# Layer 0 attention: each query and key part written to DRAM once, and repeated by the reads that fetch the rows back

## The chip, the core and the metric

The kernel runs on one core of a Trainium2 chip. A core has five engines with instruction queues of their own: PE (matrix products), DVE (vector), ACT (activation functions), POOL (general vector work, and the DMAs it issues) and SP (which here only issues DMAs). Sixteen DMA engines move data between DRAM and the on-chip memory; all queues share them. The metric is the device time of one execution in microseconds (us), lower is better.

## The reference, cut to what matters

Two transformer layers on 8 sequences (batches) of 256 rows of width 128. Each layer is a cross-attention with a residual, and a top-2 mixture of 8 experts with a residual. The change touches only the attention of layer 0: 16 heads of 8 columns each, whose scores get a hash mask.

```python
def _L0_xattn_ref(query, key, value, hash_q, hash_k, Wq, bq, Wk, bk, Wv, bv):
    q = _split_heads(query @ Wq.T + bq, B, Lq)      # 16 heads of 8
    k = _split_heads(key @ Wk.T + bk, B, Lk)
    v = _split_heads(value @ Wv.T + bv, B, Lk)
    scores = jnp.einsum('bhqd,bhkd->bhqk', q, k) / jnp.sqrt(jnp.float32(D_K))
    mask = (hash_q[:, :, :, None] != hash_k[:, :, None, :]).astype(scores.dtype) * NEG
    attn = jax.nn.softmax(scores + mask, axis=-1)
    out = jnp.einsum('bhqk,bhkd->bhqd', attn, v)
    return out.transpose(0, 2, 1, 3).reshape(B, Lq, D_MODEL)
...
x = x + _L0_xattn_ref(_layernorm(x), ctx_1024, ctx_1024, mask, mask, ...)
x = x + _L0_ffn_ref(_layernorm(x), ...)
x = x + _L1_xattn_ref(_layernorm(x), ctx_1024, ctx_1024, ...)
x = x + _L1_ffn_ref(_layernorm(x), ...)
```

## The kernel before, in words

**The operands of a score.** A float32 query or key value is split into three bf16 parts (`part`, lines 433 to 439) whose sum is the value. A float32 product is then the sum of 3 x 3 products of parts. The kernel puts all nine into one contraction: of the 128 partitions of the tiles `q9` and `k9` (one row of 16 heads x 256 positions, 8 KB in bf16, per partition), rows 0 to 71 hold (i, j, d), i and j the part numbers and d one of the 8 columns of a head. Row (i, j, d) of `q9` is part i of the query's column d, and row (i, j, d) of `k9` is part j of the key's. Rows 72 and 73 hold the hash mask (`mrow`), and rows 74 to 76 of `q9` the row maxima in three parts, `mT`, against rows of minus one in `k9`. So every part of the query stands in `q9` three times, and the same holds for the key. `q9` and `k9` have three buffers each: batch b uses number b % 3.

**prep0(b)** (line 422) makes these tiles for a batch: layer norm, the two projections, the split into parts, the value projection, four small DMAs for the mask rows (line 455), and then the rows of parts. The part tile has (column, head) on its partitions, while `q9` needs columns on partitions and heads along the row, so the rows go through a DRAM tile `rows`. For batch 0 eighteen DMAs go straight from `part` to `q9` and `k9` instead (line 467). For the others there are six writes of 192 KB (line 475), each of which writes all three parts of the query or of the key to one of the three places where they are repeated, and then two reads of 72 rows x 8 KB, 576 KB each, one into `q9` (line 478) and one into `k9` (line 479). All of these DMAs stand in SP's queue.

**The loop.** Layer 0's attention is one loop over n (lines 1083 to 1110), in which an iteration does two heads of scores for one half of the queries (`scores`, line 490 on PE, and the maximum over the keys on DVE, line 494), and, 15 iterations later, one head of probabilities (`probs`: the transposed scores with the maxima subtracted, line 521 on PE, exponential on ACT, line 528). A batch takes 16 iterations. Every iteration ends with `tick()`, which moves each generator in the list `side` on to its next `yield`; `prep0(b + 2)` is put there in iteration 2 of batch b. With its yields its mask rows are issued around the end of batch b, its writes from iteration 1 of batch b + 1 on, and its reads four ticks after the first writes.

**maxima(b, half)** (line 496) splits the maxima of eight heads into three parts, transposes them on PE, copies them on ACT (line 513) and puts them into rows 74 to 76 of `q9` by a DMA from SP, `q<-mT` (line 514). The first half of batch b (heads 0 to 7) is due in iteration 10 of b, the second half (heads 8 to 15) in iteration 2 of batch b + 1. The first `probs` of the second half, head 8, stands at iteration 7 of batch b + 1: it waits for that DMA.

**What sets the order.** PE, ACT, DVE and SP run their instructions in the order in which the program text issues them. SP's queue takes one DMA at a time: an instruction that waits holds all behind it. A read of `rows` waits until the writes of its data have landed. There are eight completion semaphores for SP's DMAs, which are used in turn, so that a DMA also waits for the eighth before it. POOL issues weight loads for later stages during the loop (`load_later`, line 250), each behind a DVE maximum.

**Another place of use.** `tails` (line 708) fills rows of a DRAM table: eight times per layer SP issues a DMA of 80 rows of 1040 float32 numbers, whose source is 16 rows repeated five times by a broadcast (line 722, `xs<-blank`, 325 KB).

Of the kernel before, what the change touches and what calls it, by code (L numbers as in the profile page):

```python
# [12 lines left out]
BF16 = mybir.dt.bfloat16  # L13
# [6 lines left out]
S = 256  # L20
QT = S // P
D = 128
H = 16
DK0 = 8
# [27 lines left out]
NPART = 3  # L52
R_MASK = NPART * NPART * DK0
# [9 lines left out]
def kernel(  # L63
# [28 lines left out]
    nc = tc.nc  # L92
# [4 lines left out]
    dp = ctx.enter_context(tc.tile_pool(name="dp", bufs=3, space=bass.MemoryType.DRAM))  # L97
# [7 lines left out]
    def bank(tag, name, dt=F32):  # L105

        if tag == "any":
            third.append(third.pop(0))
            tag = third[-1]
        return ps.tile([P, 512 * 4 // mybir.dt.size(dt)], dt, tag=tag, name=name, bufs=1 if tag in ("pv", "y") else 2)  # L110
# [77 lines left out]
    with nc.allow_non_contiguous_dma(reason="two rows of biases, once"):  # L188
        for i, src in enumerate((bq0, bk0)):
            nc.scalar.dma_start(  # L190
                out=brow[:, i, :].rearrange("o (d g j) -> o d g j", d=DK0, g=4),
                in_=src.rearrange("(o j z) g -> o z g j", o=1, z=32)[:, :DK0],
# [188 lines left out]
    def norm_T(tiles, name, rows=None, lead=2):  # L381
        n = len(tiles)
        mv = sm.tile([P, GT, 2], F32, tag="mv", name=f"mv{name}", bufs=3)
        for i, t in enumerate(tiles):
            st = sm.tile([P, 6], F32, tag="bn", name=f"st{name}_{i}", bufs=3)
            nc.vector.bn_stats(out=st, in_=t)
            nc.vector.bn_aggr(out=mv[:, i, :], in_=st)
            if i == 1 and n > 2:
                yield
        ve = sm.tile([P, GT], F32, tag="ve", name=f"ve{name}", bufs=3)  # L390
        nc.vector.tensor_scalar(ve[:, :n], mv[:, :n, 1], EPS, None, ALU.add)
        rs = sm.tile([P, GT], F32, tag="rs", name=f"rs{name}", bufs=3)
        nc.gpsimd.tensor_tensor(rs[:, :n], ve[:, :n], mhalf[:, :n], ALU.pow)
        for _ in range(lead):
            yield
        xns = []
        for i, t in enumerate(tiles):
            if rows is None:
                xn = sm.tile([P, D], F32, tag="xn", name=f"xn{name}_{i}", bufs=4)
                to = xn  # L400
            else:
                xn = rows[:, i, 0, :D]
                to, t = rows[:, i, :, :D], t.unsqueeze(1).to_broadcast([P, 2, D])
            nc.vector.tensor_scalar(to, t, mv[:, i, 0:1], rs[:, i : i + 1], ALU.subtract, ALU.mult)
            xns.append(xn)
            if i == 1 and n > 2:
                yield
        for _ in range(1 if rows is None else 2):
            yield
        pt = bank("pt", f"np{name}")  # L410
        for i, xn in enumerate(xns):
            nc.tensor.transpose(pt[:, ts(i, P)], xn, ident)
        tag, bufs = (f"xnT{n}", 2) if rows is None else (f"xnTr{n}" if n == QT else f"xnT{n}", 1)
        xnT = wk.tile([P, n * P], F32, tag=tag, name=f"xnT{name}", bufs=bufs)
        nc.scalar.copy(xnT, pt[:, : n * P])
        yield
        return xnT
# [4 lines left out]
    def prep0(b):  # L422
        q9, k9, v = q9s[b % 3], k9s[b % 3], v0s[b % 4]
        xnT = yield from norm_T(xt[b * QT : (b + 1) * QT], f"a{b}", lead=6 if b >= 2 else 2)
        pq = bank("pt", f"pq0_{b}")
        nc.tensor.matmul(pq[:, :S], lhsT=wq0_sb, rhs=xnT, start=True, stop=True)
        nc.tensor.matmul(pq[:, S:], lhsT=wk0_sb, rhs=ct[b], start=True, stop=True)
        f = wk.tile([P, 2, S], F32, tag="g2", name=f"qk{b}", bufs=5)
        nc.scalar.activation(f[:, 0, :], pq[:, :S], AF.Identity, bias=bqk[:, 0:1], scale=1.0 / math.sqrt(DK0))
        nc.scalar.activation(f[:, 1, :], pq[:, S:], AF.Identity, bias=bqk[:, 1:2])  # L430
        yield

        part = wk.tile([P, NPART, 2, S], BF16, tag="pT", name=f"part{b}")
        rest = wk.tile([P, 2, S], F32, tag="g2", name=f"rest{b}", bufs=5)
        eng = nc.vector if b < 2 else nc.gpsimd
        eng.tensor_copy(part[:, 0], f)
        eng.tensor_tensor(rest, f, part[:, 0], ALU.subtract)
        eng.tensor_copy(part[:, 1], rest)
        eng.tensor_tensor(part[:, 2], rest, part[:, 1], ALU.subtract)
        yield  # L440
        pv = bank("pt", f"pvp0_{b}")
        for t in range(QT):
            nc.tensor.matmul(pv[:, ts(t, D)], lhsT=ct[b][:, ts(t, P)], rhs=wv0_sb, start=True, stop=True)
        nc.vector.tensor_tensor(
            v[:, :, :, :DK0],
            pv[:, : QT * D].rearrange("p (t h d) -> p t h d", t=QT, d=DK0),
            bv0_sb.rearrange("p (h d) -> p h d", d=DK0).unsqueeze(1).to_broadcast([P, QT, H, DK0]),
            ALU.add,
        )
        yield  # L450
        for _ in range(2 if b >= 2 else 0):
            yield
        for t, k in ((q9, 0), (k9, 2)):
            for i in range(2):
                nc.sync.dma_start(
                    out=t[R_MASK + i : R_MASK + i + 1, :, :], in_=mrow[b * H : (b + 1) * H, k + i, :]
                )
            yield
        if b == 0:

            queues = [nc.sync, nc.scalar, nc.sync, nc.scalar, nc.gpsimd]
            for i in range(NPART):
                for j in range(NPART):
                    r = (i * NPART + j) * DK0
                    for n, t in ((0, q9), (1, k9)):
                        queues.append(queues.pop(0))
                        queues[-1].dma_start(out=t[r : r + DK0, :, :], in_=part[:, (i, j)[n], n, :])
            yield
            return

        rows = dp.tile([2, R_MASK, H, S], BF16, tag="rows", name=f"rows{b}")
        for n, by in ((0, "(i j d) h s -> j (d h) i s"), (1, "(i j d) h s -> i (d h) j s")):
            to = rows[n].rearrange(by, i=NPART, j=NPART)
            for i in range(NPART):
                nc.sync.dma_start(out=to[i], in_=part[:, :, n, :])
                if b > 1 and i:
                    yield
        nc.sync.dma_start(out=q9[:R_MASK, :, :], in_=rows[0])
        nc.sync.dma_start(out=k9[:R_MASK, :, :], in_=rows[1])
        yield  # L480

    def scores(b, i):
# [579 lines left out]

    mrow = wk.tile([P, 4, S], BF16, tag="ns", name="mrow", bufs=4)
    first = prep0(0)
    next(first)
    next(first)
# [7 lines left out]
    tick()  # L1074
    tick()
    side.append(prep0(1))
    drain()
    for i in range(3):
# [4 lines left out]
    for n in range(NS * B + LAG + 3):  # L1083
        b, i = divmod(n, NS)
        if n < NS * B:
            scores(b, i)
        if 0 <= n - LAG < H * B:
            probs(*divmod(n - LAG, H))
        g, r = divmod(n - LAG - 5, 4)
        if r == 0 and 0 <= g < 4 * B:  # L1090
            values0(*divmod(g, 4))
            if g % 2:
                side.append(finish0(g // 4, g % 4 // 2))
        if i in (HH, 0) and HH <= n <= NS * B:
            side.append(maxima((n - 1) // NS, 1 if i == 0 else 0))
        if i == 2 and b + 2 < B:
            side.append(prep0(b + 2))
        if i == 6 and b in (3, 5, 7):
            one_by_one(route(0, 2 * (b - 3), GT, nc.gpsimd))
            if b == 7:  # L1100
                one_by_one(place(0, True))
                one_by_one(route(0, NT - 2 * QT, QT))
        if n == NS * B + 8:
            side.append(keys_values(0))
        tick()
        if n == NS * B + LAG - 2:
            begin0(range(4))
            tiles0 = run0()
        if n >= NS * B + LAG:
            next(tiles0)  # L1110
# [94 lines left out]
```

## Time and profile before

| | us |
|---|---|
| median of 3 runs | 771.52 |
| lowest and highest | 765.64, 774.53 |
| the profiled execution, its own time | 772.35 |
| its span (first to last instruction) | 770.6 |

The profile is of one execution; its own time is 1.75 us over its span, and 0.8 us over the median. The busy shares of the span: PE 82%, DVE 62%, ACT 43%, POOL 42%; the granted TensorE clock was 0.904 of full speed on average.

The stages by time: set-up to 39.8 us, the loop of layer 0's attention from there to about 243 us, layer 0's experts to about 350 us, layer 1's attention to about 630 us, layer 1's experts and the combination to the end. In a line of a timeline, the first two numbers are the start and the duration in us; SPq is SP's queue and its duration is that of issuing, not of the transfer; what stands in brackets is the idle time before and what ended it. In a table of windows each engine has its busy time and its instruction count, and the last three columns are the granted clock of PE, the share of the 16 DMA engines that was busy, and GB/s.

### The profile page before, as it was taken

The numbers are of one execution on the slowest core, as the hardware profiler recorded it, in microseconds if no ns is written. First come the engines' busy times: TensorE is split into PE (matmuls) and PEld (weight loads), VectorE is DVE, ScalarE is ACT, GpSimd is POOL, SyncE is SP. The second block draws the span as 40 slices with busy tenths as digits, with TensorE's granted clock in tenths as the row PEclk, the third lists the DMA queues.
The fourth block names the chain that finished last, engine by engine and source line by source line (L and its number), as shares of the span: only waits on it lengthen the run. The fifth ranks groups of instructions, "written<-read, shape, count | busy, mean of one in ns | idle before, by whom it ended". The sixth has DMA issues, their size and how long they took to land. (4 is left out here: it accounts for less than half of the span.)

```text
span 770.6 us, 15199 instructions
## 1 busy us (share of the span) xinstructions
PE 631.4 (82%) x4781; PEld 487.1 (63%) x4781; DVE 478.3 (62%) x1804; ACT 333.0 (43%) x1028; POOL 325.9 (42%) x393
## 2 busy tenths in 40 slices
PE   2179889686876689998899999999999773979990
PEld 1135454353533679997578777777768663879990
DVE  4177787774834465554857778778786783444442
ACT  1015564443632122223675656656575550423330
POOL 4044547534060354443533444536353740454442
PEclk9956997987967799999999999999999997899995
DMA  3657876754015455662203020000000015758845
GB/s 90 57 157 220 227 188 198 166 147 121 3 63 163 118 142 154 195 168 68 68 1 90 27 77 16 16 15 16 1 15 1 15 38 173 219 157 227 232 135 170
DMA packets 72758, 83.85 MB, mean 109 GB/s; under 512 B 9648, under 2 KB 55624, under 8 KB 71672
## 3 DMA queue, kind: packets, MB, share of 16 engines
q1 hardware_dynamic: 63840, 63.79, 30.7%
q0 software_dynamic: 7600, 18.64, 8.0%
q10 hardware_dynamic: 1240, 0.46, 0.7%
q8 instruction: 39, 0.64, 0.3%
q14 instruction: 39, 0.32, 0.1%
HBM read 60.86 MB, written 30.60 MB: 119 GB/s over the span
## 5 line engine op out<-in xcount | busy, mean ns | idle before, releaser
L945 ACT ACTIVATE p<-ns,nm 128x256 f32<-128x256 f32 (+1 forms) x256 | 114.4, 450 | 33.7 <-DVE nm L934 29.0
L958 POOL TENSOR_TENSOR p<-p,rd 128x1024 f32<-128x1024 f32 (+1 forms) x63 | 92.1, 1482 | 63.6 <-DVE rd L953 62.4
L817 POOL DMA_INDIRECT ys<-yj,xj x78 | 75.1, 963 | 89.9 <-DVE yj L815 80.3
L494 DVE TENSOR_REDUCE mx<-sc 128x2 f32<-128x512 f32 x128 | 84.1, 685 | 33.2 <-PE sc L490 24.6
L656 POOL DMA_INDIRECT xs<-rows,ati x64 | 63.2, 987 | 90.8 <-DVE rows L648 45.6
L528 ACT ACTIVATE pT<-st 128x512 f32<-128x512 f32 x128 | 73.9, 596 | 60.9 <-PE st L521 56.5
L934 DVE CUSTOM_DVE_ANT_0 ns<-s,tri 128x256 f32<-128x256 f32 (+1 forms) x256 | 77.1, 350 | 0.5 <-PE s L919 0.5
L490 PE MATMUL sc<-k,q 74*128 74x256 bf16 x256 | 57.7, 315 | 19.8 <-DVE mx L494 9.4
L970 ACT COPY pT<-pt 128x512 f32<-128x512 f32 x64 | 36.9, 576 | 70.2 <-PE pt L968 70.2
L521 PE MATMUL st<-q,k 77*128 77x256 bf16 x256 | 56.8, 311 | 8.4 <-DMA q<-mT 4.4
L968 PE MATMUL pt<-ident,p 128*128 128x128 f32 x384 | 58.1, 280 | 4.7 <-POOL p L958 3.2
L968 PEld LDWEIGHTS pt<-ident,p 128*128 128x128 f32 x384 | 46.3, 143 | 23.9 <-DVE k L885 11.4
L983 PE MATMUL o<-pT,v 128*64 128x256 f32 (+1 forms) x512 | 54.2, 335 | 5.0 <-ACT pT L970 3.3
L796 DVE TENSOR_TENSOR h<-s,pu 128x256 f32<-128x256 f32 x78 | 23.9, 348 | 52.0 <-PE pu L790 21.7
L780 ACT ACTIVATE h<-ph,wj 128x128 f32<-128x128 f32 x78 | 24.5, 365 | 71.7 <-issue 51.4
L777 PE MATMUL ph<-xT,wj 128*128 128x128 f32 x312 | 47.5, 299 | 9.2 <-DVE xT L764 5.7
L919 PE MATMUL s<-k,q 64*128 64x256 f32 (+1 forms) x512 | 53.2, 338 | 0.5 <-DVE nm L934 0.5
L490 PEld LDWEIGHTS <-q 74*128 74x128 bf16 x256 | 24.8, 109 | 43.7 <-issue 38.2
L983 PEld LDWEIGHTS o<-pT,v 128*64 128x64 f32 x512 | 34.9, 137 | 23.7 <-issue 6.2
L919 PEld LDWEIGHTS s<-k,q 64*128 64x128 f32 x512 | 42.8, 186 | 10.3 <-issue 4.5
L945 ACT ACTIVATION_READ_ACCUMULATOR p<-ns,nm 128x1 f32 x256 | 49.2, 192 | 0.0
L777 PEld LDWEIGHTS ph<-xT,wj 128*128 128x128 f32 x312 | 40.7, 203 | 11.6 <-DVE xT L764 6.2
(218 smaller groups left out, 1289.8 us busy)
## 6 DMA issues: line engine op xcount, KB each, us to landing
wj<-wa SPq DMA_DIRECT2D x39, 352.0 KB
wj<-wa SPq DMA_DIRECT2D x39, 258.0 KB
rows<-part SPq DMA_DIRECT2D x42, 192.0 KB
xs<-blank SPq DMA_DIRECT2D x16, 325.0 KB
xj<-xs SPq DMA_DIRECT2D x78, 65.0 KB
yy<-ys SPq DMA_DIRECT2D x16, 256.0 KB
q<-rows SPq DMA_DIRECT2D x7, 576.0 KB
k<-rows SPq DMA_DIRECT2D x7, 576.0 KB
```

The source lines that it names most:

```text
L490: nc.tensor.matmul(sc[:, k, :], lhsT=q9s[b % 3][:R_MAX, h, ts(qt, P)], rhs=k9s[b % 3][:R_MAX, h, :], start=True, stop=True,)
L494: pace[0] = nc.vector.tensor_reduce(c0[b]["mx"][:, qt, 2 * u : 2 * u + 2], sc, AX.X, ALU.max)
L528: nc.scalar.activation(pT.rearrange("p t s -> p (t s)"), st, AF.Exp)
L656: nc.gpsimd.indirect_dma_start(out=xs[l][:, :], out_offset=to, in_=rows[:, i, k, :], in_offset=None),
L777: nc.tensor.matmul(phs[z][:, ts(i, P)], lhsT=wj[:, o : o + P], rhs=xT, start=True, stop=True)
L817: free(f"ys{l}", nc.gpsimd.indirect_dma_start(out=ys[l][:, :], out_offset=to, in_=yj, in_offset=None))
L919: nc.tensor.matmul(u["s"][a, r][:, (1 - qt) * S : (1 - qt) * S + n], lhsT=c1[b]["q"][rows, c, ts(qt, P)], rhs=c1[b]["k"][rows, c, :n], sta ...
L934: nc.vector.tensor_tensor_reduce(out=ns[:, o : o + n], in0=s[:, o : o + n], in1=tri[:, S - n :], scale=-1.0, scalar=3.0e38, op0=ALU.add, o ...
L945: nc.scalar.activation(p[:, o : o + n], ns[:, o : o + n], AF.Exp, bias=nm[:, a : a + 1], scale=-1.0, accum_out=u["sum"][:, 2 * i + a : 2 * ...
L958: eng.tensor_tensor(p, p, rd[:, :, a : a + 1].to_broadcast([P, 4, n]), ALU.mult)
L968: nc.tensor.transpose(pt[:, ts(n, P)], u["p"][:, i, (S, 0, P)[m] :][:, :P], ident)
L983: nc.tensor.matmul(o[DK1 * r : DK1 * (r + 1), a, t * P :], lhsT=v[:, t, cols], rhs=pT, start=(t == 0), stop=True, skip_group_check=True,)
```

## The change

In `prep0`, for all batches but 0: the DRAM tile `rows` becomes a third as large and holds each part of the query and of the key once. Two writes of 192 KB take the place of six, and there is one `yield` after them. The repetition moves into the reads: the query's rows come in three DMAs, one for each i, of 24 rows each, whose source is the 8 rows of part i repeated three times by a broadcast of step 0; the key's come in one DMA of 72 rows whose source is its 24 rows repeated three times. The bytes that the reads bring in are as before, 576 KB for each of the two tiles. The yields between the writes are gone.

```diff
-        rows = dp.tile([2, R_MASK, H, S], BF16, tag="rows", name=f"rows{b}")
-        for n, by in ((0, "(i j d) h s -> j (d h) i s"), (1, "(i j d) h s -> i (d h) j s")):
-            to = rows[n].rearrange(by, i=NPART, j=NPART)
-            for i in range(NPART):
-                nc.sync.dma_start(out=to[i], in_=part[:, :, n, :])
-                if b > 1 and i:
-                    yield
-        nc.sync.dma_start(out=q9[:R_MASK, :, :], in_=rows[0])
-        nc.sync.dma_start(out=k9[:R_MASK, :, :], in_=rows[1])
+        rows = dp.tile([2, NPART, DK0, H * S], BF16, tag="rows", name=f"rows{b}")
+        for n in range(2):
+            nc.sync.dma_start(
+                out=rows[n].rearrange("i d (h s) -> (d h) i s", h=H), in_=part[:, :, n, :]
+            )
+        yield
+        for i in range(NPART):
+            nc.sync.dma_start(
+                out=q9[i * NPART * DK0 : (i + 1) * NPART * DK0, :, :],
+                in_=rows[0][i].unsqueeze(0).to_broadcast([NPART, DK0, H * S]),
+            )
+        nc.sync.dma_start(
+            out=k9[:R_MASK, :, :],
+            in_=rows[1].rearrange("j d w -> (j d) w").unsqueeze(0).to_broadcast([NPART, NPART * DK0, H * S]),
+        )
         yield
```

## The prediction, made before the changed kernel was run

> **What bounds the kernel now.** I read the page's slices first, then windows of the loop of layer 0's attention (39.8 to about 243 us), then SP's and PE's timelines there.
>
> ```profile
> PE   2179889686876689998899999999999773979990
> DMA  3657876754015455662203020000000015758845
> xs<-blank SPq DMA_DIRECT2D x16, 325.0 KB
> rows<-part SPq DMA_DIRECT2D x42, 192.0 KB
> ```
>
> Slices of 19.3 us: in the loop (slices 3 to 12) PE is mostly at 8 to 9 tenths and the DMA engines at 5 to 8. The stage runs at PE's pace, and since PE takes its instructions in order, a wait on PE is paid in full unless PE would have idled later.
>
> ```profile
> core 0: us, PE busy (x) PEld busy (x) DVE busy (x) ACT busy (x) POOL busy (x), PEclk, DMA share, GB/s
> 43.00:44.00 1.00, 0.16 (x1) 0.00 (x0) 0.93 (x6) 0.00 (x0) 0.37 (x1) 0.50 0.76 197
> 56.50:76.40 19.90, 19.67 (x133) 11.55 (x131) 14.05 (x37) 11.40 (x22) 9.40 (x15) 0.66 0.79 219
> 76.40:92.20 15.80, 15.30 (x148) 9.41 (x147) 13.46 (x38) 10.65 (x22) 8.37 (x12) 1.00 0.84 243
> 634.00:644.00 10.00, 8.22 (x69) 6.59 (x65) 4.87 (x17) 1.55 (x3) 0.72 (x1) 1.00 0.32 127
> ```
>
> Last three columns: granted clock, busy share of the 16 DMA engines, GB/s. At 43 us little but a read of 72 plain rows runs: share 0.76, so about 12 engines of 16, at 197/12 = 16.4 GB/s each. From 634 to 644 us it is almost only `xs<-blank`, whose source is a broadcast of five: share 0.32, so 5 engines, at 127/5 = 25 GB/s each. The other eleven idle while SP's queue has more for them.
>
> ```profile
> 57.78 1.58 SPq L475 DMA_DIRECT2D rows<-part  x3
> 60.44 0.80 SPq L514 DMA_DIRECT2D q<-mT  x1
> 61.28 1.60 SPq L475 DMA_DIRECT2D rows<-part  x3
> 64.02 0.33 SPq L478 DMA_DIRECT2D q<-rows  x1
> 66.28 0.32 SPq L479 DMA_DIRECT2D k<-rows  x1
> 86.19 0.31 SPq L479 DMA_DIRECT2D k<-rows  x1
> 89.89 0.78 SPq L514 DMA_DIRECT2D q<-mT  x1
> ```
>
> ```profile
> 65.58 0.64 PE L521 MATMUL st<-q,k 77*128 77x256 bf16 x2
> 95.86 0.38 PE L521 MATMUL st<-q,k 77*128 77x256 bf16 x2 [2.78 <-DMA k<-mrow]
> 154.19 0.39 PE L521 MATMUL st<-q,k 77*128 77x256 bf16 x2 [2.94 <-DMA q<-mT]
> 167.31 0.39 PE L521 MATMUL st<-q,k 77*128 77x256 bf16 x2 [1.48 <-DMA q<-mT]
> ```
>
> The SP rows are one preparation (batch 2) and the end of the next. `q<-mT` at 60.44 is the second half of batch 0's maxima; head 8 of batch 0 needs it, at 65.58. It stands between the writes, ahead of the reads. `q<-mT` at 89.89 is a first half; it stands behind the k read of 86.19, and head 0 of batch 2 starts only at 95.86, after 2.78 us of idling (the page puts that on `k<-mrow`, long done). So an `mT` behind the big reads lands when they have, about 5.9 us after its issue here, while one with nothing big ahead (152.06, needed at 154.19) takes 2.1.
>
> **The change part by part.**
>
> *Four writes fewer for each of 7 batches.* A write keeps all DMA engines busy for about 0.7 us: at 40 to 42 us the share is 1.05 with 290 GB/s, and 192 KB at that rate is 0.68 us. So 28 x 0.7 = 19 us of DMA time go, and 28 issues of 0.5 us on SP. Neither is what PE waits for: no score of batches 1 to 7 waits for `q<-rows` or `k<-rows`. Worth 0 by itself; the cover is the slack of 9 to 10 us between a k read's issue (66.28) and its first score (76.38).
>
> *The reads move up.* They followed the sixth write, two to four iterations later; now they follow the second. In the built program SP's order for a batch is: four mask rows, two writes, four reads, then the second half's `mT`. Before, the `mT` stood ahead of the reads (even ahead of the last three writes). So what waits behind the reads changes from the first half's `mT` to the second half's. Gain: the waits of 2.78 and 1.48 us, about 4 us.
>
> *The reads themselves.* Here row and rule part from the plain estimate. Row: 2 x 576 KB = 1.18 MB at 197 GB/s is 6.0 us. But a broadcast source ran on 5 engines for a broadcast of five. The Trainium skill, "DMA: Bandwidth & Descriptors", section "Rules for kernel authors", says why: a DMA runs on the largest number of engines, up to 16, that divides the slowest dimension of both access patterns, so a leading broadcast of c copies confines it to c engines. The row of 0.32 agrees for c = 5. All four new reads lead with a broadcast of 3: three engines, 144/3 = 48 rows of 8 KB each. At 25 GB/s a row is 0.33 us: 16 us. Bounds: at 16.4 GB/s per engine (the 43 us row) 24 us; nothing in the trace moves more than about 25 GB/s on an engine, so hardly under 15. I take 16, as few engines are the nearer row, plus 2 us for POOL's loads, which share these engines (estimate: the loop's 219 GB/s less the rows' traffic leaves about 2 MB in 20 us, 5 us of each engine; PE's wait stops the loads, which go behind DVE's maxima, so I take less than half). The skill's page also says that these are the lowest-numbered engines; an `mT`, 3 rows, then uses the same three, and queues behind the reads as it did at 89.89.
>
> *When the second half lands.* With W the issue of a batch's first write: the first read can go once that write has landed, 3.2 us (a k read follows the last write by 2.4 to 3.4 us); 1.7 us to the first data (the q read of 41.39 is seen at 43); 18 us of reads. The `mT` lands at W + 23. Head 8 of the batch in question starts, before, after W by:
>
> W = 57.78, 79.07, 95.00, 119.19, 147.82, 168.21; head 8 = 65.58, 84.11, 104.60, 129.36, 154.19, 177.63; distances 7.8, 5.0, 9.6, 10.2, 6.4, 9.4, together 48.4.
>
> Six stalls of PE, 6 x 23 - 48.4 = 90 us. Behind the waiting `st` on PE stand the next scores, so DVE, ACT and POOL's pacing stop with it. Batches 6 and 7 have no preparation and no stall.
>
> *Start.* Batch 1's reads begin at about 42.5 and hold the three engines to about 58.5. Behind them in SP's queue are the nine `k<-minus`, the eighth of which waits for the k read's semaphore (eight in turn), and then batch 0's first `mT`, issued at about 60 instead of 53.74, landed at 62; head 0 of batch 0 started at 56.13: +6 us. The first scores, at 39.8, are untouched.
>
> *Clock.* After each stall PE restarts at half speed. Rule: "TensorE: Matmul & The Clock Gate", Part 1, the clock halves when PE idles for more than about 3.4 us, and a stretch of PE work would take up to twice as long. Row: the 16 score iterations at 0.66 mostly (56.56 to 75.43) took 18.9 us, those at 1.00 (76.38 to 92.2) 15.8; half speed costs 0.2 to 0.3 us an iteration, not double. By the rule 6 x 5 us or more, by the row about 6 x 1.5 = 9 us; I take the row.
>
> *Given back.* DVE and POOL catch up during stalls: PE's waits of 6.5 us before 186.8 (ACT's `oT`) and 2.7 at 141.6 (DVE) may go. -8 us.
>
> The tails, layer 1 and the experts are as before and start later by the sum: 90 + 6 + 9 - 4 - 8 = **+93 us**. The profiled execution is 772.35, so 865; it lies 0.8 over the median, which changes nothing.
>
> **The rivals.**
>
> *Twelve engines after all* (the compiler or queue spreads the repeated rows over their 24 or 72). Then only the order changes: reads 6 + 2 us, `mT` at W + 13.2, stalls 79 - 48 = 31, less 4 and less 8, no start term: about +19, 791 us. For: the destination has 24 and 72 rows. Against: `xs<-blank` has 80 rows and still ran on 5 engines.
>
> *Faster:* the reads are early and harmless, and only the waits at the first halves go: -4 to -7, 767 us. One mechanism: the second `mT` has to land before head 8, within 5 to 10 us of W, of which 5.2 are latency; that leaves at most 5 us for 1.18 MB, 236 GB/s from these reads alone, decided at that rate. Against: no read of rows came near it (197).
>
> *Three engines at the slow rate:* 24 us of reads instead of 16, 6 x 8 = 48 more and 8 at the start: 921 us. For: 8 KB rows took the slow rate on twelve engines. Against: five engines with repeated rows had 25 GB/s each, and at 43 us the twelve may have slowed each other, which three would do less.
>
> **How the numbers follow.** Three engines near 25 GB/s 0.82: 865. Slow rate 0.09: 921. Twelve engines 0.05: 791. Faster or unchanged 0.04: 767. The likeliest gives the time. Its own range is 822 (15 us, no interference by POOL, a larger share given back) to 910; to leave out no more than 2 in 10, the upper end goes to 915, and the low end stays at 820, as twelve engines and the harmless cases together are 0.09. About 1% (8 us) is what a measurement of this kernel tells from no change; faster 0.03, within 1% 0.02, slower 0.95.
>
> **What would show it.** In the loop of the new profile: DMA share near 0.2 to 0.3 for some 16 us after each pair of writes, at about 75 GB/s; PE idle at `st<-q,k` six times for 12 to 18 us until `q<-mT`, at heads 8 of batches 0 to 5, and about 6 us at the first head; no such wait in batches 6 and 7; half clock after each. Wrong if the reads show a share of 0.7, or if the waits are at the scores instead, or if the stages after the loop change length.

## The result: slower by an eighth

The changed kernel takes 867.09 us (median of four runs, 865.18 to 868.97). The kernel before, run beside it, takes 773.02 us (765.64 to 778.54). The ratio is 1.125, with an interval of 1.116 to 1.134. It is not the quotient of the two medians because it leaves out a slow run of the kernel before, 778.54 (the mean of its other three runs is 770.56). The prediction was 865 us in a range of 820 to 915. The profiled execution took 867.82 us, over a span of 866.1 us, which is 95.5 us more than the span before.

The page of the changed kernel: busy tenths in 40 slices of 21.7 us, then two of the costliest groups (busy time and mean of one; after the second bar, the idle time before them and what ended most of it).

```profile
PE   2243825544373876779998999999999977579990
...
PEclk9555858667776967899999999999999999698996
DMA  3523314151412014456623022000000002656865
...
L500 DVE TENSOR_REDUCE mx<-sc 128x2 f32<-128x512 f32 x128 | 83.7, 683 | 128.0 <-PE sc L496 126.3
L527 PE MATMUL st<-q,k 77*128 77x256 bf16 x256 | 57.4, 313 | 109.8 <-DMA q<-mT 108.7
```

The loop of layer 0's attention (slices 2 to 15) shows PE at 8 tenths in two slices and at 2 to 7 in the others. PE and the DMA engines are both low in most of them: nobody is the bottleneck by its amount of work. The line numbers are six higher than before: L527 is the `st` matmul of `probs`. It idled for 108.7 us until `q<-mT` had landed. DVE idles with it (128.0 us), because the scores that it reduces stand behind the waiting `st` on PE.

PE's timeline, lines with that wait (start, duration, and in brackets the idle time before and what ended it):

```profile
64.33 0.59 PE L527 MATMUL st<-q,k 77*128 77x256 bf16 x2 [9.14 <-DMA q<-mT]
88.07 0.60 PE L527 MATMUL st<-q,k 77*128 77x256 bf16 x2 [15.13 <-DMA q<-mT]
123.49 0.61 PE L527 MATMUL st<-q,k 77*128 77x256 bf16 x2 [17.04 <-DMA q<-mT]
160.53 0.61 PE L527 MATMUL st<-q,k 77*128 77x256 bf16 x2 [17.75 <-DMA q<-mT]
203.50 0.61 PE L527 MATMUL st<-q,k 77*128 77x256 bf16 x2 [17.91 <-DMA q<-mT]
241.74 0.61 PE L527 MATMUL st<-q,k 77*128 77x256 bf16 x2 [17.17 <-DMA q<-mT]
278.50 0.61 PE L527 MATMUL st<-q,k 77*128 77x256 bf16 x2 [14.56 <-DMA q<-mT]
```

The first is head 0 of batch 0. The six others are heads 8 of batches 0 to 5, together 99.6 us. Batches 6 and 7, which have no preparation of another batch beside them, have no such line.

SP's timeline around the first of the six, with the queue's order as the prediction gave it: two writes, three reads of the query's rows, one of the key's, then the `mT` that head 8 at 88.07 waits for, 16.8 us after its issue.

```profile
42.58 19.57 SPq L333 DMA_DIRECT2D k<-minus  x9
...
62.25 0.78 SPq L520 DMA_DIRECT2D q<-mT  x1
...
65.58 1.06 SPq L473 DMA_DIRECT2D rows<-part  x2
67.83 2.25 SPq L478 DMA_DIRECT2D q<-rows  x3
70.50 0.68 SPq L482 DMA_DIRECT2D k<-rows  x1
71.28 0.74 SPq L520 DMA_DIRECT2D q<-mT  x1
```

Windows of the changed kernel, two within the waits and three behind the first of them (last three columns: granted clock, busy share of the 16 DMA engines, GB/s):

```profile
76.00:87.00 11.00, 0.00 (x0) 0.00 (x0) 0.00 (x0) 0.00 (x0) 0.00 (x0) 0.50 0.19 78
110.00:121.00 11.00, 0.00 (x0) 0.00 (x0) 0.00 (x0) 0.00 (x0) 0.00 (x0) 0.50 0.19 80
...
88.00:91.00 3.00, 2.93 (x22) 1.32 (x22) 1.75 (x7) 1.19 (x2) 0.56 (x1) 0.50 0.00 0
91.00:94.00 3.00, 3.00 (x22) 2.14 (x18) 1.87 (x6) 2.04 (x4) 0.00 (x0) 0.87 0.28 87
94.00:97.00 3.00, 3.00 (x33) 1.85 (x32) 1.51 (x4) 2.04 (x5) 2.23 (x3) 1.00 0.27 90
```

For 11 us no compute engine does anything, while 0.19 of 16 engines, that is three, move 78 to 80 GB/s, about 26 GB/s each. Thirteen DMA engines stand by.

Where the 95.5 us of span went can be added up from the timelines: until the first `st` (56.34 before, 64.33 after) 8.0; from there to the last `st` (242.4 before, 335.9 after) 186.1 become 271.6, which is 85.5; from there to the end 528.2 become 530.2, which is 2.0.

### The profile page after: what moved, and what is told of

It reads as the page before. It is cut to its first block, busy times and chain, and to the rows that moved or that the text cites. A ratio compares the mean times of both kernels' runs of the same rounds, so it can differ in the third digit from the quotient of the medians.

```text
span 866.1 us, 15178 instructions
## 1 busy us (share of the span) xinstructions
PE 632.6 (73%) x4781; PEld 487.5 (56%) x4781; DVE 478.1 (55%) x1804; ACT 332.0 (38%) x1028; POOL 325.9 (38%) x393
## 5 line engine op out<-in xcount | busy, mean ns | idle before, releaser
L500 DVE TENSOR_REDUCE mx<-sc 128x2 f32<-128x512 f32 x128 | 83.7, 683 | 128.0 <-PE sc L496 126.3
L527 PE MATMUL st<-q,k 77*128 77x256 bf16 x256 | 57.4, 313 | 109.8 <-DMA q<-mT 108.7
L527 PEld LDWEIGHTS <-k 77*128 77x128 bf16 x256 | 27.3, 110 | 121.7 <-DMA q<-mT 101.2
L496 PE MATMUL sc<-k,q 74*128 74x256 bf16 x256 | 57.5, 315 | 18.9 <-DVE mx L500 11.6
```

The lines of the kernel that those rows point to most:

```text
L496: nc.tensor.matmul(sc[:, k, :], lhsT=q9s[b % 3][:R_MAX, h, ts(qt, P)], rhs=k9s[b % 3][:R_MAX, h, :], start=True, stop=True,)
L500: pace[0] = nc.vector.tensor_reduce(c0[b]["mx"][:, qt, 2 * u : 2 * u + 2], sc, AX.X, ALU.max)
L527: nc.tensor.matmul(st[:, ts(t, S)], lhsT=k9s[b % 3][:R_ALL, h, ts(t, P)], rhs=q9s[b % 3][:R_ALL, h, :], start=True, stop=True,)
```

## The experiments

Each kernel computes the whole. Its ratio is to runs of the kernel before on the same chip in the same session; that kernel took 768.67 us beside the first four, 749.12 beside the next three and 771.92 beside the last, so the ratios are what to compare, not the times.

### The mT from another queue

```diff
-        nc.sync.dma_start(out=q9s[b % 3][R_MAX:R_ALL, ts(hf, HH), :], in_=mT)
+        nc.scalar.dma_start(out=q9s[b % 3][R_MAX:R_ALL, ts(hf, HH), :], in_=mT)
```

> The changed kernel, with the maxima rows q<-mT issued from ACT's queue instead of SP's; reads, engines and places as in the changed kernel. Theory (the second half's q<-mT is held because it stands behind three-engine reads in the same queue): from another queue it lands in 2 to 4 us although the reads run on the same engines, so the six waits of 101 us at head 8 shrink below 10 in all. Left are about 7 us at the first head (k<-minus still stands behind batch 1's reads) and new, small waits of the scores for reads that land 22 us after the first write (they are needed 17 to 26 us after it: some 10 us in all): 780 to 795 us. Rival (three crowded DMA engines hold every DMA that uses them, whatever its queue): still 855 to 870.

Measured: 825.96 us, ratio 1.071 (1.061 to 1.082), between the two ranges and in neither. PE's waits from 30 to 345 us (total, times, longest):

```profile
PE sc L496 <- DMA q<-mrow: 25.2, 2, 18.9
PE st L527 <- DMA q<-mT: 23.9, 8, 6.4
PE sc L496 <- DMA k<-rows: 12.1, 1, 12.1
```

The stalls at `st` shrank from 108.7 to 31.2 us: the 23.9, and 7.3 at the first head, which stand under `k<-minus` in this profile. So most of the wait was the place in the queue. Not all of it: an `mT` that PE waited for took 3.3 to 9.7 us here from its issue by ACT to the waiting `st` (105.03 to 111.22 and 130.44 to 140.14, for instance), against 15.3 to 21.6 us in SP's queue, and against the 2 to 4 us that were expected. The rival, that the crowded engines hold every DMA, fits that part; no run here singles it out.

The scores now wait for rows in the loop, 18.9 and 12.1 us (6.3 of the first line are at the start, where the kernel before waits too, 8.0 us). SP's timeline of this kernel shows why, for the first of the two, which ends at 98.63:

```profile
70.85 1.06 SPq L473 DMA_DIRECT2D rows<-part  x2
78.62 2.25 SPq L478 DMA_DIRECT2D q<-rows  x3
80.97 0.69 SPq L482 DMA_DIRECT2D k<-rows  x1
```

The q reads go out 7.8 us after the writes; in the changed kernel it was 2.3 us (65.58 and 67.83), and the writes themselves were 5 us earlier. Something holds SP's queue now. The last experiment looks at that.

### The reads four ticks later

```diff
-        yield
+        for _ in range(4 if b > 1 else 1):
+            yield
         for i in range(NPART):
```

> The changed kernel with its four reads issued four ticks after the two writes, as the kernel before had them, so behind the second half's q<-mT; still three engines. Theory: the waits at head 8 go, and come back smaller at head 0, where the first half's q<-mT now stands behind reads that take about 19 us from their issue and is needed about 12 us after it: six waits of 2 to 10 us, some 40 us, and 7 at the start: 815 to 830 us. Rival (the cost is the length of the reads alone, wherever they stand): 860 to 870. Rival (the cost is the place alone): 770 to 780.

Measured: 827.53 us, ratio 1.073 (1.064 to 1.083), as expected. The second half's `mT` is now ahead of the reads, and the first half's behind them. PE's timeline has the stalls at heads 0 instead of heads 8: five of 7.2 to 11.1 us, 47.0 together, and 9.0 at the start. The first three of the five:

```profile
91.18 0.59 PE L528 MATMUL st<-q,k 77*128 77x256 bf16 x2 [9.22 <-DMA q<-mT]
120.97 0.59 PE L528 MATMUL st<-q,k 77*128 77x256 bf16 x2 [11.09 <-DMA q<-mT]
151.81 0.61 PE L528 MATMUL st<-q,k 77*128 77x256 bf16 x2 [7.22 <-DMA q<-mT]
```

So long reads find an `mT` to hold up in either place. A batch has two of them, and takes about 20 us undisturbed (56.34 to 95.86 for two batches in the kernel before). Reads that last until 20 us after their first issue (67.83 to 88.07 in the changed kernel) find no gap between the two.

### The repetition inside

```diff
-        for i in range(NPART):
+        for j in range(NPART):
             nc.sync.dma_start(
-                out=q9[i * NPART * DK0 : (i + 1) * NPART * DK0, :, :],
-                in_=rows[0][i].unsqueeze(0).to_broadcast([NPART, DK0, H * S]),
+                out=q9[j * NPART * DK0 : (j + 1) * NPART * DK0, :, :],
+                in_=rows[0].rearrange("i d w -> d i w"),
             )
...
-            in_=rows[1].rearrange("j d w -> (j d) w").unsqueeze(0).to_broadcast([NPART, NPART * DK0, H * S]),
+            in_=rows[1].rearrange("j d w -> (j d) w").unsqueeze(1).to_broadcast([NPART * DK0, NPART, H * S]),
```

The rows of a tile stand in the order (j, d, i), so that a read's leading count is 8 or 24 and not 3; the sum over the rows is the same.

> The changed kernel with the rows of q9 and k9 in another order, (j, d, i) with i fastest, so that the repetition is the inner dimension of the source: the same bytes, the same rows read three times from the same DRAM tile, the same place in SP's queue, but q on eight engines and k on twelve. Theory (the number of engines is what makes the reads long): reads of 6 to 8 us, DMA share above 0.5 while they run, q<-mT lands about 13 us after the first write; six waits of some 3 to 8 us: 785 to 795 us. Rival (reading the same DRAM rows three times is slow in itself): 855 to 870.

Measured: 811.52 us, ratio 1.054 (1.046 to 1.063). This lies under the rival's range and over the theory's. Two windows of the reads of batch 3, the second mostly of the key's:

```profile
93.00:95.00 2.00, 0.33 (x2) 0.04 (x1) 1.09 (x2) 0.58 (x1) 0.73 (x2) 1.00 0.55 186
95.00:101.00 6.00, 0.00 (x0) 0.00 (x0) 0.00 (x0) 0.00 (x0) 0.00 (x0) 0.61 0.69 213
```

In all, 186 to 213 GB/s move instead of 78. A part of that are POOL's loads: of the 1.28 MB of the second window SP's queue, with the reads, has 0.85, or 142 GB/s, and its packets take 46% of the 16 engines' time. In the changed kernel, from 76 to 87 us, SP's queue has 76 GB/s and 18%. The key's source is as repeated as there. So the zero step did no harm behind a long count; it is its standing first that costs. What remains is in PE's timeline:

```profile
74.62 0.61 PE L527 MATMUL st<-q,k 77*128 77x256 bf16 x2 [8.70 <-DMA q<-mT]
101.76 0.60 PE L527 MATMUL st<-q,k 77*128 77x256 bf16 x2 [8.43 <-DMA q<-mT]
130.63 0.61 PE L527 MATMUL st<-q,k 77*128 77x256 bf16 x2 [10.10 <-DMA q<-mT]
163.79 0.61 PE L527 MATMUL st<-q,k 77*128 77x256 bf16 x2 [9.96 <-DMA q<-mT]
```

The first writes of these four batches went out at 58.83, 88.43, 114.63 and 146.16, so PE goes on with the `mT` 13.3 to 17.6 us after them, where the estimate for many engines was 13.2. A fifth stall is of 9.38 us. At head 8 of batch 5 PE stands for another 7.29 us, which the profile puts down to no releaser ("issue").

### Three engines without repetition

The kernel before, with one spare row of DRAM after every 24, so that a plain read has a leading count of 3:

```diff
-        rows = dp.tile([2, R_MASK, H, S], BF16, tag="rows", name=f"rows{b}")
+        rows = dp.tile([2, NPART, NPART * DK0 + 1, H, S], BF16, tag="rows", name=f"rows{b}")
...
-        nc.sync.dma_start(out=q9[:R_MASK, :, :], in_=rows[0])
-        nc.sync.dma_start(out=k9[:R_MASK, :, :], in_=rows[1])
+        for n, t in ((0, q9), (1, k9)):
+            nc.sync.dma_start(
+                out=t[:R_MASK, :, :], in_=rows[n][:, : NPART * DK0].rearrange("i r h s -> i r (h s)")
+            )
```

> The kernel before with its DRAM tile padded to 25 rows for each 24, so that each of its two reads has three blocks of 24 rows as slowest dimension: no repetition in the reads, six writes and the places as before, but three engines. Theory: as slow as the changed kernel with late reads, waits at head 0 and at the start: 815 to 835 us, reads at about 75 GB/s. Rival (repetition is what is slow): 770 to 778.

Measured: 840.19 us, ratio 1.090 (1.080 to 1.100), a little over the theory's range and far from the rival's. A window of its loop (as above), and a wait of SP's queue from 40 to 240 us (total, times, longest):

```profile
91.00:97.00 6.00, 0.00 (x0) 0.00 (x0) 0.00 (x0) 0.00 (x0) 0.00 (x0) 0.50 0.19 74
...
SPq L475 <- DMA k<-rows: 29.9, 4, 8.3
```

While a k read runs (issued at 77.84) the share is 0.19 again, three engines of 16. Nothing is repeated and the reads are in their old place, and yet the kernel loses 70 us. PE waits 74.4 us at `st` for `q<-mT`, against 56.7 in the kernel with late reads above. Writes are held up too: three of them, from 87.40 us on, take 9.78 us to be issued, where three took 1.58 in the kernel before. The third has the completion semaphore of the k read of 77.84, the eighth DMA before it in SP's queue, and waits for that read.

### Order alone

The kernel before, its six writes and plain reads without yields between them, so that they all go out ahead of the second half's `mT`:

```diff
                 nc.sync.dma_start(out=to[i], in_=part[:, :, n, :])
-                if b > 1 and i:
-                    yield
```

> The kernel before with one thing changed: all six writes and both reads of a batch go out at once, ahead of the second half's mT; the reads are plain, on twelve engines, and nothing is repeated by them. Theory (place in SP's queue costs by itself): the mT lands about 15 to 17 us after the first write, six stalls at head 8 of 6 to 9 us: 800 to 820, ratio 1.04 to 1.065. Rival (only the three engines cost; with twelve the place of the mT is harmless): 765 to 780.

Measured: 788.94 us beside 749.12, ratio 1.057 (1.052 to 1.062; the quotient of the medians is 1.053): the theory by its ratio, while its microseconds were reckoned from about 770. PE's timeline, the first four of six stalls:

```profile
71.05 0.61 PE L519 MATMUL st<-q,k 77*128 77x256 bf16 x2 [8.13 <-DMA q<-mT]
99.27 0.60 PE L519 MATMUL st<-q,k 77*128 77x256 bf16 x2 [9.63 <-DMA q<-mT]
127.34 0.61 PE L519 MATMUL st<-q,k 77*128 77x256 bf16 x2 [9.82 <-DMA q<-mT]
159.10 0.61 PE L519 MATMUL st<-q,k 77*128 77x256 bf16 x2 [6.01 <-DMA q<-mT]
```

The stalls are at the same heads as those of the kernel with the repetition inside, and add up to 46.8 us in six, where that one has 46.6 in five and the 7.29 besides. The two kernels differ in their writes and in what the reads repeat; with many engines and the early place in common, they give the same loss, 5.7 and 5.4%.

### Both undone, the fewer writes kept

The kernel with the repetition inside, with the reads four ticks later as above.

> Two writes for a batch as in the changed kernel, but the repetition stands inside (8 and 12 engines a read) and the reads go four steps later, so that the second half's mT is issued ahead of them, as before the change. Theory (the loss is the product of two things, few engines and a mT behind the reads, and the fewer writes are worth nothing, since no score waits for them): within 1% of the kernel before, 762 to 782, with no wait of the st matmuls for q<-mT over 4 us. Rival 1 (repeating by the read, or its smaller pieces, costs in itself): 795 or more. Rival 2 (the 19 us of DMA time that four writes fewer save do reach the end): 745 to 760.

Measured: 745.87 us beside 749.12, ratio 0.9955 (0.9925 to 0.9985). PE's waits at `st` in the loop:

```profile
PE st L528 <- DMA q<-mT: 5.6, 2, 2.9
```

The loss is gone, and rival 1 with it. The number itself lies in rival 2's range, but only because the kernel before took 749.12 here: the expectation's 762 to 782 for "within 1%" is reckoned from 772, so rival 2 meant 1.6 to 3.5% less, and it is 0.2 to 0.8%. That is what four writes fewer and the repeated reads are worth together, less than the 1% that the prediction takes as its bound, although the interval leaves out 1. This is the quickest of the kernels measured. If the expectation's "product of two things" is taken to say that neither costs anything without the other, it is not borne out: the few engines in the old place cost 7.3%, the early place on many engines 5.7%. The two add up to about the changed kernel's 12.5%. In each an `mT` stands behind the reads; what differs is which one, and for how long.

### Early reads on many engines, and the mT from ACT

The kernel with the repetition inside, with the edit of the first experiment.

> The reads in the changed kernel's place with the repetition inside (8 and 12 engines; 811 with the mT in SP's queue), and the mT issued from ACT's queue. Theory (what was left of the loss, about 43 us, is the mT waiting in SP's queue behind the reads): stalls at head 8 mostly gone, 772 to 795. Rival (the mT's packets wait on the same engines whichever queue they come from, or SP's DMAs wait for the semaphores that ACT's now share): 800 to 820, with waits at the scores.

Measured: 756.21 us beside 749.12, ratio 1.011 (1.007 to 1.014). The theory's range, put against the 768.67 of the session before, was 1.004 to 1.034; the rival's began at 1.041. PE's waits in the loop:

```profile
PE sc L496 <- DMA q<-mrow: 18.4, 2, 12.3
...
PE st L527 <- DMA q<-mT: 4.2, 2, 2.7
```

From 46.6 us in SP's queue to 4.2 us in ACT's, beside the same reads on the same engines: here the wait was one of queue order. The waits at the scores, which the rival named, are there too: 12.3 us in the loop (the other 6.0 of that line are at the start) and 3.6 more for a k read, less than what is gained.

### What ACT's queue costs by itself

The kernel before, with the edit of the first experiment.

> The kernel before with the mT issued from ACT's queue and nothing else changed; six writes, plain reads, reads in the old place. It splits what is left of the loss (ratio 1.011) when the early reads have many engines and the mT comes from ACT. Theory (that rest is the price of ACT's queue itself: SP's DMAs wait for completion semaphores that they now share with ACT's, so reads and mask rows come late at the scores): ratio 1.003 to 1.02, with waits of the sc matmuls for q<-mrow or k<-rows of 5 us or more in the loop. Rival (the rest is the reads' early place on the same engines): ratio 0.985 to 1.0, no such waits.

Measured: 797.23 us, ratio 1.033 (1.026 to 1.040): the theory's sign and its waits, but more than its range. The scores waited twice in the loop, 12.75 and 11.71 us (the profile puts them down to the writes of the rows that they read through `q9` and `k9`); the last `st` stands 26.2 us later than in the kernel before (268.5 against 242.3). The wait of PE, and SP's own waits from 40 to 220 us, show the resource:

```profile
PE sc L490 <- DMA rows<-part: 24.5, 2, 12.7
...
SPq L475 <- DMA q<-mT: 24.2, 4, 8.7
...
SPq L333 <- DMA q<-mT: 10.1, 1, 10.1
```

L475 are the writes of rows, L333 the `k<-minus` rows: neither uses anything of an `mT`. They wait for one because in this program the eight completion semaphores are given out in turn over both queues. The write that waited 8.7 us went out at 75.03, and has the semaphore of the `mT` that ACT issued only at 72.98: SP waited until ACT had come to that `mT` and it had landed. So an `mT` in ACT's queue doesn't stand behind SP's reads, but SP's DMAs wait for it. The first experiment has the same pair: its q read of 78.62 has the semaphore of the `mT` that ACT issued at 76.29. How much of the last 1.1% of the kernel above is this price and how much is the reads' early place was not told apart: this kernel, with six writes, loses 3.3%, that one 1.1% in all.

## Why the prediction was right, term by term

- **Three engines near 25 GB/s, 0.33 us a row.** Shown: share 0.19, 78 to 80 GB/s, 26 GB/s an engine. The rule on the leading count, read off `xs<-blank`, held for 3 as for 5. Three plain groups of rows ran at the same share of 0.19 and lost no less than three copies in the same place (1.090 against 1.073), so it is the count and not the copying. Which three engines they are no trace shows. The rival with the slow rate falls by this row. The 2 us for POOL's loads were about right: from 69.5 to 76 us, where the loads move 0.52 MB, SP's queue moves 0.32 MB, or 49 GB/s; from 76 to 87 us, almost without them, it moves 76 GB/s. At that rate the first stretch would have taken 4.2 us instead of 6.5. No run was made without the loads.
- **The mT at W + 23.** Heads 8 start 22.5, 21.8, 23.7, 27.6, 21.1 and 22.6 us after the first write of the preparation beside them (88.07 - 65.58 and so on): 23.2 on average.
- **Stalls of 90 us.** 99.6. The landing was right; what was off is the 48.4 subtracted. PE came to the six heads 39.7 us after W in sum and not 48.4 (15.13 before 88.07 is 72.94, 7.4 after 65.58; in the same way 4.8, 5.9, 9.7, 3.9 and 8.0). Of the 8.7 between, 2.94 is a wait for `q<-mT` that one of these heads already had before (154.19): the prediction counted it as PE's own distance, and it shows that only 96.7 of the 99.6 are new. The other 5.8 stay unexplained.
- **Start, 6 us.** 8.0. The nine `k<-minus` hold the queue for 19.57 us, where they took 7.72, the `mT` goes out at 62.25 and head 0 starts at 64.33. With the repetition inside, the first `st` is at 57.0, against 56.3 before: the term belongs to the three engines.
- **Clock, 9 us: wrong.** About 0. The clock does stay at half for some 3 us after a stall (the windows above), and then rises to full. But the kernel before spends part of its loop at a low clock too. Weighted over the seven stretches between stalls the clock was 0.81 in the changed kernel, against 0.82 before, and PE's busy time from the first `st` to the last (the first figure behind the length; before, then after) hardly differs:

```profile
56.30:242.70 186.40, 152.97 (x1183) 88.34 (x1180) 125.91 (x366) 92.14 (x182) 82.80 (x130) 0.82 0.54 149
64.30:336.20 271.90, 153.61 (x1180) 89.16 (x1180) 125.54 (x363) 91.77 (x182) 80.81 (x127) 0.72 0.26 83
```

The 0.72 has the stalls in it. A stall's price in clock was counted as if the work that follows had run at full clock otherwise.
- **Waits at the first halves, -4.** The waits of 2.78 and 1.48 us are gone, 4.3 us.
- **Given back, -8.** -7.7: the other waits of PE in the loop add up to 25.3 before and 17.6 after. The waits of PE in the loop, before and then after:

```profile
PE po L549 <- ACT oT L544: 13.4, 7, 6.5
PE sc L490 <- DVE mx L494: 5.9, 8, 2.7
PE st L521 <- DMA q<-mT: 4.4, 2, 2.9
PE st L521 <- DMA k<-mrow: 2.8, 1, 2.8
```

```profile
PE st L527 <- DMA q<-mT: 99.6, 6, 17.9
PE sc L496 <- DVE mx L500: 8.1, 13, 2.2
PE po L555 <- ACT oT L550: 7.6, 8, 5.8
```

- **Later stages unchanged.** They take 2.0 us more, which nothing here explains. The prediction named a change of length there as a sign against it; 2.0 us is 0.4% of these stages, and runs of the kernel before differ by more (765.64 to 774.53).

Together: 96.7 + 8.0 - 4.3 - 7.7 + 2.0 and 0.8 of remainder make 95.5 us. The path, the wait and the rate were as predicted. That 93 came out within 2.5 us is partly luck: the clock's 9 us too much stood in for stalls that were put 7 us too short, and for 2 us each at the start and in the later stages.

**The rival with twelve engines.** The reason given against it was weaker than it looked: `xs<-blank` writes its 80 rows as five groups of 16 (line 722), so its destination leads with five as well and did not tell what 24 or 72 rows there would do. The changed kernel, with 24 and 72, tells it. The rival was priced at +19 us and would have been wrong as a number: the two kernels with reads on many engines in the early place lose 5.4 and 5.7%, some 42 us. Its landing of W + 13.2 was measured as 15.4 on average over five batches (15.8, 13.3, 16.0, 17.6 and 14.1), which makes 6 x 2.2 = 13 us, and the distances too long by about 9 make the rest. **The faster rival** needed the reads to be done before head 8; no kernel here had its reads early and free of charge. **The writes at zero:** right within 1%, as the ratio 0.9955 says.

## What to carry to other kernels

A DMA that repeats rows should have the repetition behind a long count, not ahead of it: here SP's reads took 18% or 46% of the 16 engines' time by the order of two dimensions, and the row that tells is the DMA share in a window where little else runs. When a large transfer is moved up in a queue, list what small DMA is behind it now and who waits for that: all seven stalls of the changed kernel are waits for twelve kilobytes. Saved traffic that nobody waited for was worth less than 1% here, so an edit that saves it has to leave queue order alone.

## What was not expected of the hardware

A DMA from another queue isn't free of the first queue: with the `mT` issued by ACT, SP's writes waited 24.2 us in sum for `mT`s through shared completion semaphores, and the kernel before became 3.3% slower by that edit alone. And the data of two queues do pass each other on the same engines, but not freely: behind the many-engine reads in SP's queue the `mT` cost PE 46.6 us, beside them in ACT's 4.2 us; beside three-engine reads an `mT` from ACT that PE waited for still took 3.3 to 9.7 us. The rate of one DMA engine also depended on the company: 26 GB/s on three, and 213/(0.69 x 16) = 19 GB/s on the eleven busy ones in the kernel with the repetition inside, POOL's loads among them.
